# Two cross-attentions: the root and the reciprocal of the image scores' norms as one power on GpSimd

## The chip, the core and the metric

The kernel runs on one core of a Trainium2 chip. The metric is the device time of one execution in microseconds (us), the median of several runs. The engines are named as in the profile: PE is TensorE's matmuls (PEld its weight loads), DVE is VectorE, ACT is ScalarE, POOL is GpSimd and SP is SyncE, which here only issues DMAs. A name such as L864 is line 864 of the kernel before.

## The reference

Two cross-attention layers follow one another on `x` of shape (64, 256, 320): 64 batches, 256 tokens, 20 heads of 16 channels. Each batch has 77 context rows of 512 channels. All arithmetic is float32.

The first layer is a plain softmax attention over all 77 rows. The second layer takes 73 rows as text and the last 4 as image tokens. The text part is a plain softmax attention. The image part adds to its scores a similarity between the context that the text attention has gathered and the image tokens, both divided by their norms:

```python
qsem = jnp.einsum('bhst,bte->bhse', probs_t, text_ehs)
qsem = _l2norm(qsem)            # x / max(sqrt(sum(x * x)), 1e-12)
ip_n = _l2norm(ip_ehs)
sem = jnp.einsum('bhse,bne->bhsn', qsem, ip_n)
fused = attn_scores + 0.5 * sem
probs_ip = jax.nn.softmax(fused, axis=-1) * spatial_mask[None, None, :, None]
out = text_out + probs_ip @ v_ip
```

Each layer ends in a projection, a bias and the residual.

## The kernel before

Everything lies on chip with channels on the partitions. The 64 batches go in 32 pairs p. A pair and layer is cut into ten units: five for each batch b of the pair, each of 128 tokens and eight heads (the last unit of five holds both token halves of the last four heads). One main loop over steps g handles one unit of layer 0 and one unit of layer 1 of an earlier pair (13 steps behind), so that a pair takes ten steps; k = g mod 10 is the place in such a round. The order of the instructions on TensorE, VectorE, ScalarE and GpSimd is the order in which the program writes them: `keep_order` pins it (SP's only up to step 13). Into each step the program puts other work by its k (`fillers`): projections, queries, keys, value rows.

A step does the following.
- TensorE writes one four-bank PSUM tile `sc` (there is only one, so the next step's matmuls wait until the last reader is done): the semantic products of the unit before last of layer 1 (`semantics`, L763 and L770), then the scores of the new units (`scores`, L649).
- VectorE takes the maximum `mx` (L667) and the difference `w` (L669) for each layer, then `prod` (L781, L784) from the semantic products.
- ScalarE takes the exponentials (L677 for layer 0, L680 and L681 for layer 1), copies `sums` out of `sc` (L1048), and copies the transposed weights `pt` and `pr` out of PSUM (L719, L720, L738, L739).
- TensorE transposes the weights (L712, L713).
- VectorE sums and inverts layer 0's weights (`sm`, L694, L695); GpSimd multiplies them (`parts`, L699). GpSimd also copies layer 1's image scores aside (`att`, L684).
- VectorE reduces `prod` to the unit's part of `nrm` (L1121), the squared length of the gathered context. The length itself is never built: the kernel uses a Gram matrix of the context rows, which `gram` (L505 to L511) prepares a batch at a time and sends through DRAM.

With the last unit of a batch, which falls on k = 9 for b = 0 and on k = 4 for b = 1 (the `ends` steps, 64 in all), come the norms of the whole batch, 128 partitions by 40 columns (two token halves by 20 heads):
- `image_squares` (L859, L860, VectorE) bounds the squared length from below; `text_output` (L833 on VectorE, then three products by `by_head`, L851, on GpSimd) scales the text output into `an`.
- At the very end of that step, `image_norm` (L864, L866, ScalarE) takes the square root with a constant factor, and after it one dummy exponential of a single column. An ACT_TABLE_LOAD stands ahead of each.
- In the next step, `image_scores` inverts the root on VectorE (L872) and GpSimd multiplies and adds (`num`, L873, L874).
- One step on, `image_shifted` takes the maximum (`most`, L879, VectorE) and subtracts it (L880, GpSimd), and `image_exponential` (L883) follows. In the third step `image_weights` normalizes (L890 to L892, and L851 again).
- Transposes (L904) and `outputs` (L917, L929) bring the image part into the projection.

`image_norms` (L332 to L340) runs once near the start: it inverts the norms of all image tokens, 128 by 256 columns, into `rip`, by which `gram` scales the image columns (L509). At the start and in the last steps `keep_busy` (L748) has TensorE transpose the identity where it would otherwise pause.

Of the kernel before, what the change touches and what calls it, by code (L numbers as in the profile page):

```python
# [8 lines left out]
F32 = mybir.dt.float32  # L9
AF = mybir.ActivationFunctionType  # L10
ALU = mybir.AluOpType
# [3 lines left out]
H = 20  # L15
# [7 lines left out]
P = 128  # L23
# [25 lines left out]
SCALE = D**-0.5  # L49
SEM = 0.5  # L50
# [21 lines left out]
def tile_two_cross_attentions(ctx: ExitStack, tc: tile.TileContext, a: dict, out: bass.AP):  # L72
# [35 lines left out]
    nc = tc.nc  # L108
# [5 lines left out]
    const = ctx.enter_context(tc.tile_pool(name="const", bufs=1))  # L114
# [192 lines left out]
    rip = const.tile([P, NIP * NB], F32, tag="rip", name="rip")  # L307
# [24 lines left out]
    def image_norms():  # L332
        sq = wkip.rearrange("p k c -> p (k c)")[:, : KE * NIP * NB].rearrange("p (k t) -> p k t", k=KE)
        nc.vector.tensor_mul(sq, cip, cip)
        ps = pms.tile([P, 512], F32, tag="ms", name="ss_ps")
        for k in range(KE):
            nc.tensor.matmul(ps[:, : NIP * NB], ones, sq[:, k, :], start=(k == 0), stop=(k == KE - 1))
        nc.vector.tensor_scalar_max(rip, ps[:, : NIP * NB], EPS * EPS)
        nc.scalar.activation(rip, rip, AF.Sqrt)
        nc.vector.reciprocal(rip, rip)  # L340


# [493 lines left out]
            lasts[p] = big.tile([P, 2, 2, H - HT, D], F32, tag="an_last", name=f"an_last{p}", bufs=1)  # L836
        by_head((an[:, 0], lasts[p][:, :, b], an[:, 1]), sums[:, :, NIP : NIP + D], rec)

    one = const.tile([P, 1], F32, tag="one", name="one")

    def by_head(to, t, factor):

# [18 lines left out]

    def image_norm(p, b):
        r = stats[p, b][2]
        nc.scalar.activation(r, r, AF.Sqrt, scale=(SCALE / SEM) ** 2)  # L864

        nc.scalar.activation(one, r[:, :1], AF.Exp, scale=0.0)  # L866

    def image_scores(p, b):

        att, sums, r = stats[p, b]  # L870
        num = nums[p, b] = small.tile(full, F32, tag="num", name=f"num{p}_{b}", bufs=2)
        nc.vector.reciprocal(r, r)  # L872
        nc.gpsimd.tensor_mul(num, sums[:, :, :NIP], r.unsqueeze(2).broadcast_to(full))  # L873
        nc.gpsimd.tensor_add(num, num, att)  # L874

# [65 lines left out]
    def fillers(k, p):  # L941
# [58 lines left out]
        elif k == 6:  # L1000
# [5 lines left out]
            if p == 0:  # L1006
                add(0, p, image_norms)
            else:
                add(1, p, keys, 1, p, 1)
# [42 lines left out]
    for g in range(NP * NU + LAG + 12):  # L1052
# [66 lines left out]
        if before1:  # L1119
            q, b, u = before1[:3]  # L1120
            nc.vector.tensor_reduce(eight(stats[q, b][2], u), prod, AX.X, ALU.add)  # L1121
            if ends:
                image_squares(q, b)
                text_output(q, b)
                later[g + 1] = [(image_scores, (q, b))]
                middle[g + 2] = (image_shifted, (q, b))
                between[g + 2] = [(image_exponential, (q, b))]
                (early if b else later)[g + 3] = [(image_weights, (q, b))]
# [10 lines left out]
        if ends:  # L1139
            image_norm(*before1[:2])  # L1140
# [54 lines left out]
```

## Time and profile before

| What | Value |
|---|---|
| Median of 3 runs | 2466.0 us (2465.18 to 2466.5) |
| The profiled execution's own time | 2466.13 us |
| Its span in the profile | 2464.4 us, 97472 instructions |
| Mean granted TensorE clock | 0.997 |
| ScalarE: table loads at L864 and L866 | 64 and 64, 1283 ns each |
| ScalarE: root L864, dummy L866 | 64 and 64, mean 237 and 203 ns |
| VectorE: reciprocal L872 | 64, mean 354 ns |

In the profile, "busy" is the time in which an engine executes, and a wait is put down to the instruction that came last of those waited for. A group line reads: line, engine, operation, output<-inputs, shapes, count, then busy us, mean ns of one, and after the second bar the engine's idle time just before such instructions with what ended it. A timeline line reads: start (us from the span's start), us, engine, line, operation, output<-inputs, shapes, count, and in brackets the idle time before it. The chain of work is followed back from the last instruction, at each step to what released it.

### The profile page before, as it was taken

To read this page: it belongs to the slowest core of one execution; us is meant where nothing else is said; L and a number is where in the kernel's file an instruction comes from. 1 tells how busy PE (TensorE), PEld (TensorE's weight loads), DVE (VectorE), ACT (ScalarE), POOL (GpSimd) and SP (SyncE) were. 2 spreads that over 40 slices of the span, in tenths; PEclk is the share of its full clock that TensorE was granted. 3 is DMA by queue.
4 is the path that set the end of the run, shared out by engine and by line. 5 is a ranking of instruction groups with operands and counts; after the bars stand their busy time and mean duration, and the time that the engine had idled before them with its cause. 6 is when DMAs were issued, how large, how long until landed. Compare 5 with 4: busy or idle time off the path is not lost.

```text
span 2464.4 us, 97472 instructions
## 1 busy us (share of the span) xinstructions
PE 2394.9 (97%) x41118; PEld 1848.5 (75%) x41118; DVE 1986.4 (81%) x3673; ACT 1482.6 (60%) x3742; POOL 1207.8 (49%) x2651
## 2 busy tenths in 40 slices
PE   8899999999999999999999999999999999999888
PEld 6677777777777777777777777777777777777666
DVE  3588788888888888888888888888888888888764
ACT  3466666666666665666666666666666666666543
POOL 2455454555445545445555445555455555455532
PEclk9999999999999999999999999999999999999999
DMA  6212111112211112211111211111211111211000
GB/s 177 71 28 59 55 48 49 50 48 59 65 42 47 48 49 58 66 42 48 48 51 54 67 43 47 48 50 54 67 44 47 48 50 54 65 40 35 23 22 25
DMA packets 163447, 128.79 MB, mean 52 GB/s; under 512 B 65860, under 2 KB 146628, under 8 KB 163012
## 3 DMA queue, kind: packets, MB, share of 16 engines
q1 hardware_dynamic: 162148, 121.42, 17.4%
q8 instruction: 325, 5.32, 0.9%
q10 hardware_dynamic: 864, 1.15, 0.2%
q14 instruction: 110, 0.90, 0.1%
HBM read 83.43 MB, written 36.62 MB: 49 GB/s over the span
## 4 chain that ended last, share of the span: by engine, by line
PE 85%; DVE 10%; ACT 3%; issue 1%; POOL 0%; DMA 0%; DVEq 0%; POOLq 0%; SPq 0%; ACTq 0%
PE tr L712 11%; PE sc L763 10%; PE o_ps L537 9%; PE q_ps L537 9%; PE sc L649 7%; PE v_ps L395 4%; DVE w L669 4%; PE sc L770 4%; PE o_ps L622 4%; DVE mx L667 3%; PE k_ps L353 3%; PE pv L798 3%; PE o_ps L547 3%; PE q_ps L565 3%; PE q_ps L547 3%; PE pv L803 2%
## 5 line engine op out<-in xcount | busy, mean ns | idle before, releaser
L667 DVE TENSOR_REDUCE mx<-sc 128x8 f32<-128x584 f32 (+1 forms) x640 | 496.6, 776 | 333.4 <-PE sc L649 331.1
L699 POOL TENSOR_TENSOR parts<-w,sm 128x512 f32<-128x512 f32 (+1 forms) x640 | 441.1, 711 | 513.7 <-ACT parts L681 236.9
L669 DVE TENSOR_TENSOR w<-sc,mx 128x616 f32<-128x616 f32 x640 | 511.8, 800 | 73.1 <-DVE mx L667 1.4
L712 PE MATMUL tr<-ident,parts 128*128 128x128 f32 x2560 | 407.9, 282 | 10.4 <-ACT pt L719 6.4
L719 ACT COPY pt<-tr 128x512 f32<-128x512 f32 x320 | 187.3, 585 | 325.0 <-PE tr L712 325.0
L712 PEld LDWEIGHTS tr<-ident,parts 128*128 128x128 f32 x2560 | 284.2, 140 | 129.7 <-issue 72.8
L677 ACT ACTIVATE w<-w 128x616 f32<-128x616 f32 x320 | 229.9, 718 | 140.5 <-DVE w L669 136.8
L763 PEld LDWEIGHTS sc<-gv,pt 64*64 64x64 f32 x10240 | 233.0, 133 | 104.7 <-ACT sums L1048 51.3
L684 POOL COPY att<-w 128x32 f32<-128x32 f32 x320 | 67.6, 211 | 485.6 <-DVE w L669 485.6
L763 PE MATMUL sc<-gv,pt 64*64 64x94 f32 x10240 | 277.2, 245 | 22.9 <-ACT sums L1048 22.2
L694 DVE TENSOR_REDUCE sm<-w 128x8 f32<-128x616 f32 x320 | 250.9, 784 | 14.4 <-ACT w L677 14.3
L649 PE MATMUL sc<-kbd,q 32*64 32x154 f32 x10240 | 247.3, 293 | 1.1 <-ACT q L592 1.0
L1048 ACT COPY sums<-sc 128x168 f32<-128x168 f32 x320 | 96.6, 302 | 227.6 <-DVE prod L784 225.9
L537 PE MATMUL o_ps<-aT,wo 128*128 128x256 f32 x1024 | 231.8, 379 | 0.7 <-ACT aT L934 0.7
L537 PE MATMUL q_ps<-x,wq 128*128 128x256 f32 x1024 | 231.6, 379 | 0.0
L1121 DVE TENSOR_REDUCE nrm<-prod 128x8 f32<-128x584 f32 x320 | 226.7, 709 | 0.3
L781 DVE TENSOR_TENSOR prod<-sc,parts 128x512 f32<-128x512 f32 x320 | 217.8, 681 | 2.8 <-PE sc L770 2.8
L537 PEld LDWEIGHTS o_ps<-aT,wo 128*128 128x128 f32 x1024 | 189.6, 190 | 24.4 <-ACT aT L934 1.1
L537 PEld LDWEIGHTS q_ps<-x,wq 128*128 128x128 f32 x1024 | 189.6, 190 | 23.1
L680 ACT ACTIVATE parts<-w 128x512 f32<-128x512 f32 x320 | 206.3, 645 | 0.0
L738 ACT COPY pt<-tr 128x512 f32<-128x512 f32 x256 | 150.8, 589 | 67.1 <-PE tr L712 67.0
L395 PE MATMUL v_ps<-wv,cf 128*128 128x320 f32 (+1 forms) x624 | 179.2, 433 | 0.0
(142 smaller groups left out, 4387.0 us busy)
## 6 DMA issues: line engine op xcount, KB each, us to landing
out_dram<-x SPq DMA_DIRECT2D x64, 256.0 KB
x<-in_x_dram SPq DMA_DIRECT2D x31, 512.0 KB
vm<-v_rows SPq DMA_DIRECT2D x64, 160.0 KB
ct<-in_ctx_dram SPq DMA_DIRECT2D x32, 308.0 KB
cf<-in_ctx_dram SPq DMA_DIRECT2D x38, 256.0 KB
vr<-v_rows SPq DMA_DIRECT2D x64, 130.0 KB
v_rows<-vs SPq DMA_DIRECT2D x38, 192.0 KB
vq<-v_rows SPq DMA_DIRECT2D x128, 48.0 KB
```

The source lines that it names most:

```text
L395: nc.tensor.matmul(ps[:n, :C], cfs[i][:, k, :n], wv[l][:, k, :], start=(k == 0), stop=(k == KE - 1))
L537: nc.tensor.matmul(ps[b][:, m, :], w[:, k, m * P : (m + 1) * P], main[:, k, b * S : (b + 1) * S], start=(k == 0 and m == 0), stop=False,)
L649: nc.tensor.matmul(ps[c, r, 2 * T * l : 2 * T * (l + 1)], tokens[rows, c], kbd[rows, part].rearrange("p e t -> p (e t)"), start=start, sto ...
L667: nc.vector.tensor_reduce(mx, sc[:, :, :, :nt], AX.X, ALU.max)
L669: nc.vector.tensor_tensor(w, sc, mx.unsqueeze(3).broadcast_to([P, 4, 2, T]), ALU.subtract)
L677: nc.scalar.activation(w, w, AF.Exp, scale=SCALE)
L694: nc.vector.tensor_reduce(sm, w, AX.X, ALU.add)
L699: nc.gpsimd.tensor_tensor(two[:, 8 * t0 : 8 * t1].rearrange("p (h t) -> p h t", h=8), w[:, :, t0:t1], sm.unsqueeze(2).broadcast_to([P, 8, ...
L712: nc.tensor.transpose(ps[:, i, :], flat[:, i * P : (i + 1) * P], ident)
L763: nc.tensor.matmul(ps[c, i % 2 * 2 + j, at : at + GV], pt[half_rows, i, c], gv[b][half_rows, part, i, :], start=start and i < 2, stop=False,)
L781: nc.vector.tensor_tensor(prod[:, :, :, :M], sm[:, :, :, :M], w[:, :4].rearrange("p (e a) j t -> p (a j) e t", e=2), ALU.mult)
L1121: nc.vector.tensor_reduce(eight(stats[q, b][2], u), prod, AX.X, ALU.add)
```

## The change

The root with the constant factor, the dummy exponential and the reciprocal become one GpSimd instruction, which raises the squared lengths to the power -0.5, given as a tile of constants. It stands where the root stood: at the end of the `ends` step, after that step's GpSimd work. The constant factor moves into `image_norms`, so that `rip` carries it; there the root and the reciprocal stay as they were.

```diff
         nc.vector.tensor_scalar_max(rip, ps[:, : NIP * NB], EPS * EPS)
-        nc.scalar.activation(rip, rip, AF.Sqrt)
+        nc.scalar.activation(rip, rip, AF.Sqrt, scale=(SCALE / SEM) ** 2)
         nc.vector.reciprocal(rip, rip)
...
-    one = const.tile([P, 1], F32, tag="one", name="one")
+    power = const.tile([P, 2 * H], F32, tag="power", name="power")
+    nc.gpsimd.memset(power, -0.5)
...
     def image_norm(p, b):
         r = stats[p, b][2]
-        nc.scalar.activation(r, r, AF.Sqrt, scale=(SCALE / SEM) ** 2)
-
-        nc.scalar.activation(one, r[:, :1], AF.Exp, scale=0.0)
+        nc.gpsimd.tensor_tensor(r, r, power, ALU.pow)
...
         num = nums[p, b] = small.tile(full, F32, tag="num", name=f"num{p}_{b}", bufs=2)
-        nc.vector.reciprocal(r, r)
         nc.gpsimd.tensor_mul(num, sums[:, :, :NIP], r.unsqueeze(2).broadcast_to(full))
         nc.gpsimd.tensor_add(num, num, att)
```

In the order of instructions, ScalarE loses 128 table loads, 64 roots and 64 dummies, VectorE 64 reciprocals; GpSimd gains 64 powers and one memset; TensorE and SP keep theirs, and all others stay in the same order.

## The prediction

> **What bounds the kernel now.** I read the page's first parts, then the chain of work, then the groups by engine, and last the timeline around the edited steps.
>
> ```profile
> PE 2394.9 (97%) x41118; PEld 1848.5 (75%) x41118; DVE 1986.4 (81%) x3673; ACT 1482.6 (60%) x3742; POOL 1207.8 (49%) x2651
> PE 85%; DVE 10%; ACT 3%; issue 1%; POOL 0%; DMA 0%; DVEq 0%; POOLq 0%; SPq 0%; ACTq 0%
> ```
>
> TensorE is busy 97% of the span at a granted clock of 0.9 or more in all 40 slices, and 85% of the chain is its own. A full round of ten steps lasts 72.8 us in the timeline (from one first `sc` matmul to the next tenth). Step 4, where the second batch's norms come due, lasts 8.22 us (1204.31 to 1212.53) and the chain in it is TensorE alone; step 5, after it, lasts 6.2 us and its chain is VectorE: `mx`, `w`, `mx`, `w`, `prod`, ScalarE's `sums`, and back to the matmuls. So what the edit frees on ScalarE counts only where one of these two chains waits for it.
>
> The groups that the edit touches, from the groups by engine with shapes apart:
>
> ```profile
> L864 ACT ACT_TABLE_LOAD x64 | 82.1, 1283 | 1.1
> L866 ACT ACT_TABLE_LOAD x64 | 82.1, 1283 | 1.1
> L872 DVE RECIPROCAL nrm<-nrm 128x40 f32<-128x40 f32 x64 | 22.6, 354 | 2.0 <-ACT one L866 2.0
> L892 POOL TENSOR_TENSOR imx<-imx,smask 128x40 f32<-128x40 f32 x64 | 16.3, 255 | 5.5 <-DVE imx L891 3.0
> L254 POOL TENSOR_TENSOR head_mask<-head_mask 128x2 f32<-128x2 f32 x1 | 0.2, 195 | 0.1
> ```
>
> **Removed.** At 64 places ScalarE loses load, root, load and dummy exponential: 1283 + 237 + 1283 + 203 = 3006 ns, 192 us in all. VectorE loses 64 reciprocals of 354 ns, 22.6 us. That is 9% of the span, and nearly all of it is covered. At the places after step 4, VectorE's `mx` idles 0.38 us for TensorE after the reciprocal's step, so the 0.35 us only lengthens that idle time; at those after step 9 TensorE runs without a gap (0.04 us idle in step 0). The key matmuls at 1215.20 wait 0.32 us for a copy that the load held up, but in a step that VectorE's chain sets, so I count nothing for it (29 such waits, 9.6 us in all; a rival below). What must go on hiding these savings is TensorE's queries and output projections, and at the kernel's two ends that cover is thin:
>
> ```profile
> 148.78 0.41 PE L712 MATMUL tr<-ident,parts 128*128 128x128 f32 x2 [1.51 <-ACT pt L719]
> 2318.59 0.66 PE L712 MATMUL tr<-ident,parts 128*128 128x128 f32 x2 [2.14 <-ACT pt L719]
> 2391.28 0.98 PE L748 MATMUL busy<-ident 128*128 128x128 f32 x7 [2.00 <-ACT pt L719]
> 2440.44 0.63 POOL L851 TENSOR_TENSOR an<-sums,rec 128x256 f32<-128x256 f32 x1
> 2441.34 0.40 DVE L872 RECIPROCAL nrm<-nrm 128x40 f32<-128x40 f32 x1 [2.00 <-ACT one L866]
> 2441.82 0.49 POOL L873 TENSOR_TENSOR num<-sums,nrm 128x160 f32<-128x160 f32 x1 [0.75 <-DVE nrm L872]
> ```
>
> In the first three, TensorE stands idle for the copy `pt`, which stands behind the two loads. What is late next decides each gain.
> - At 148.8: without loads the transposes could start near 147.3, but `sums` ends near 150.95 on VectorE's chain, and the next `sc` starts at 151.32 now. Gain 0.4 us.
> - At 2318.6: the copy could start at 2316.4 instead of 2317.9, and the four transposes, the gram and the value matmuls would not run slowed after the pause (1.09, 1.24 and 1.00 us against 0.60, 0.70 and 0.64 in a full round). Next late is `sums`, which can end at 2320.7; `sc` starts at 2323.23 now. Gain 2.5 us.
> - At 2391.3: the transposes end at 2389.17, the copy starts at 2390.66. Gain 1.4 us.
> - The tail: GpSimd ends `an` at 2441.07 and starts `num` at 2441.82, after load, dummy and reciprocal. That gap of 0.75 us, less some 0.05 for a start on its own engine's result, is 0.7 us given back, and the power, x us long, stands in its place. Everything after it is serial (`most`, the subtraction, four `vip` products on GpSimd, weights, transposes, projection), so the tail changes by x - 0.7.
>
> **Added.** 64 powers of 128x40 on GpSimd, each x us, queued behind the three `an` products at the end of a step; behind it wait, in GpSimd's queue, the copy `att`, the two `parts` products, `num` and the gram's scaling with its DMA on SP. The power itself waits for nothing: the root's input is ready before `rec`, for which `an` already waits. `num` now waits for GpSimd's own result instead of VectorE's.
>
> No row shows GpSimd computing a power. From below: the multiply of the same shape, 0.255 us (L892). From above: as if each of the 40 columns cost what GpSimd's smallest product does, 0.195 us (L254): 7.8 us. Between them: L699's 128x512 takes 1051 ns in the same view, so a column of one multiply costs (1051 - 255) / 472 = 1.69 ns beside a fixed 0.19. I assume some 30 dependent steps a column (logarithm, product, exponential): 30 x 40 x 1.69 ns + 0.19 = 2.2 us. This is an estimate, nearer to the low row, since the fixed part is paid once an instruction. I take x = 2.2 and keep both ends.
>
> Its cover, from the timeline of a full round:
>
> ```profile
> 1214.24 0.63 POOL L851 TENSOR_TENSOR an<-sums,rec 128x256 f32<-128x256 f32 x1
> 1217.88 0.21 POOL L684 COPY att<-w 128x32 f32<-128x32 f32 x1 [3.01 <-DVE w L669]
> 1219.66 1.38 POOL L699 TENSOR_TENSOR parts<-w,sm 128x512 f32<-128x512 f32 x2 [1.57 <-ACT parts L681]
> 1221.57 0.52 POOL L874 TENSOR_TENSOR num<-num,att 128x160 f32<-128x160 f32 x1
> 1223.98 0.31 DVE L879 TENSOR_REDUCE most<-num 128x40 f32<-128x160 f32 x1
> ```
>
> GpSimd is free from 1214.87; less the copy, 4.5 us pass before `parts` is due. If that is overrun, `num` ends 1.9 us ahead of `most`, which sits in VectorE's chain. So up to x = 6.4 us nothing moves, and each microsecond beyond costs 32 times that. After step 9 the same reading gives 4.45 + 1.6, and 0.86 more because TensorE sets that step: 6.9 us. At 2391 the third gain survives to about x = 4.1.
>
> The rest has one answer: one memset of 128x40 at the start lies ahead of a wait of 5.6 us for `kT`; the factor in the image keys' root adds no instruction; the root there keeps its two loads.
>
> **A rule against the change.** No row shows a pause on GpSimd at the first use of an operation. The Trainium skill (GPSIMD Engine Reference, Instruction dispatch) says that the first call of a freshly loaded kernel pays about 6 us for its code. No run here shows it; if it held once, at 148 us, the sum would grow by some 2 us, and if it held at every place, x would be past 8.
>
> **And one that overstates the gain.** After a load that begins at 2316.47 and takes 1.28 us, the next activation starts at 2317.76, 0.01 us later. The skill (ScalarE: Activation LUTs, What ACT_TABLE_LOAD costs) adds a drain of about 1.38 us to each switch, which the trace does not have; by it the freed time would be, as an estimate, some 370 us instead of 192, and as well covered.
>
> **The sum.** The profiled execution took 2466.13 us, 1.7 beside its span of 2464.4; the median of the three is 2466.0. -0.4 - 2.5 - 1.4 + (2.2 - 0.7) = -2.8, so 2466.1 - 2.8 = 2463.3 us. About 0.2%, 4.9 us, is what a measurement of this kernel can tell from no change, so this lies within it.
>
> **Rivals.**
> - GpSimd becomes the bound. Beyond x = 6.4 the late `num` stops `most`, and with it `prod`, `sums` and the next step's matmuls. At x = 7.8: 32 x 1.4 + 32 x 0.9 = 74 us in the rounds, 7.1 in the tail, less 2.9 (the third gain is gone): 2544 us. For it: a power may be computed in many more steps than 30. Against it: that needs some three times my estimate. Chance 0.30; 0.12 of that lies up to x = 7.2, which gives 26 + 10 + 6.5 - 2.9 = 39.7, 2506 us.
> - The freed ScalarE time shows in every round after all. If the 29 waits of the key matmuls (9.6 us) count in full, 2463.3 - 9.6 = 2453.7 us; half of it gives 2458.5. For it: a hidden pause of TensorE may count. Against it: the 0.38 us by which VectorE idles there for the matmuls, while the same chain came to them through `sums`. With the cheapest power alone, x = 0.255, the time is 2461.4. Together 0.17 for a time more than 4.9 us shorter.
> - The change not doing what it says is excluded: by the order of instructions 128 loads, 64 roots, 64 dummies and 64 reciprocals are gone, and each engine keeps the rest in order.
>
> **Numbers.** My forecast, within 0.2%, has 0.53: x between 0.3 and 6.4, its own range 2461 to 2470. The range takes in half of the faster rival and the slower one to x = 7.2: 2458.5 to 2506, which leaves out 0.18 above and a little below.
>
> **What would show it.** No table load but the first three; the power's mean near 2.2 us on GpSimd; rounds of 72.8 us unchanged; TensorE's waits at 148, 2318 and 2391 gone; `num` in the tail later by about 1.5 us relative to `an`. Wrong: a power above 6.4 us, with `most` waiting for `num` in every round, or step 5 shorter than 6.2 us.

## The result and the profile after

The changed kernel is slower: 2488.53 us in the median of 4 runs (2487.58 to 2488.71), against 2465.59 us (2465.15 to 2466.5) for the kernel before beside it. The ratio is 1.0092 [1.0074, 1.0109], a loss of 22.9 us. The forecast was 2463.3 us, no measurable change; the time lies in the range given, on the side of the rival "GpSimd becomes the bound". The profiled execution took 2488.71 us with a span of 2487.0, so 22.6 us more span than before, at a mean granted clock of 0.995 instead of 0.997.

From the page of the changed kernel, the engines' busy times, the shares of the chain that ended last, and the group of the new instruction:

```profile
PE 2396.9 (96%) x41118; PEld 1851.5 (74%) x41118; DVE 1975.4 (79%) x3609; ACT 1297.9 (52%) x3486; POOL 1629.8 (66%) x2716
...
PE 82%; DVE 10%; POOL 5%; ACT 2%; issue 1%; DMA 0%; DVEq 0%; SPq 0%; POOLq 0%; ACTq 0%
...
L865 POOL TENSOR_TENSOR nrm<-nrm,power 128x40 f32<-128x40 f32 x64 | 434.6, 6790 | 0.0
```

ScalarE lost 184.7 us of work and VectorE 11.0; TensorE's stayed within 2 us. GpSimd gained 422 us: one power takes 6.79 us, three times the forecast's 2.2. GpSimd is still busy only two thirds of the span, but it holds 5% of the chain where it held none. The view of waits, for VectorE (waiting line, releaser, then us in total, times, longest us), says where it came in:

```profile
DVE most L877 <- POOL num L872: 22.3, 33, 9.7
DVE w L669 <- POOL att L684: 4.6, 5, 2.4
```

Before, `most` waited for `num` once, 1.2 us in the tail. Now it does 33 times: 9.7 us in the tail, where nothing else is left to do, and 12.6 us over 32 places elsewhere. Of these 32, 29 stand in step 1, after a power of step 9, with 0.37 us each in most rounds; step 1 itself is no longer for it (7.28 us as before). In step 6, after a power of step 4, VectorE idles only some 0.13 us for `num`, and this view counts waits from 0.15 us on. The five waits for `att` are few, but the longest of them, 2.4 us, falls in the last round. The timeline of GpSimd and VectorE in the same full round as in the prediction (the lines are L852 for `an`, L871 and L872 for `num`, L877 for `most` in the changed kernel):

```profile
1220.25 0.63 POOL L852 TENSOR_TENSOR an<-sums,rec 128x256 f32<-128x256 f32 x1
1220.84 6.79 POOL L865 TENSOR_TENSOR nrm<-nrm,power 128x40 f32<-128x40 f32 x1
...
1227.59 0.20 POOL L684 COPY att<-w 128x32 f32<-128x32 f32 x1
1227.76 1.37 POOL L699 TENSOR_TENSOR parts<-w,sm 128x512 f32<-128x512 f32 x2
1229.29 0.80 DVE L669 TENSOR_TENSOR w<-sc,mx 128x616 f32<-128x616 f32 x1
1229.65 0.52 POOL L872 TENSOR_TENSOR num<-num,att 128x160 f32<-128x160 f32 x1
1230.21 0.32 DVE L877 TENSOR_REDUCE most<-num 128x40 f32<-128x160 f32 x1
1230.45 0.68 DVE L781 TENSOR_TENSOR prod<-sc,parts 128x512 f32<-128x512 f32 x1
```

Read it downwards: the power runs from 1220.84 to 1227.6, and the copy, the two `parts` products and `num` follow without a gap. `num` ends at 1230.17 and `most` starts at 1230.21, after VectorE's `w` has ended at 1230.09. Counted from the step's first `sc` matmul, `most` starts at 5.26 us instead of 5.04 in the median of the full rounds. Behind `most`, on VectorE, stands `prod`, which sets when the next step's matmuls start. Before, `num` ended 1.9 us ahead of `most`.

Where the 22.6 us went, from the lengths of the same step in both kernels (a step starts with its first `sc` matmul):

| Place | Change of the span, us |
|---|---|
| Ahead of the first `sc` matmul and in the first two rounds (from -2.0 to +0.5 in sum in the runs below, whatever the edit) | +0.2 |
| The third round, the first behind a power | +1.6 |
| 28 full rounds, 73.13 us instead of 72.77 each in the median | +9.4 |
| The round before the last | +0.8 |
| The last round | +4.0 |
| Tail, after the last `sc` matmul | +6.6 |

In a full round step 6 grew by 0.22 us (6.69 instead of 6.47), step 3 by 0.10, and step 0 by 0.03. Over the 28 rounds that is 5.0 us in step 6 and 3.3 in step 3.

Step 3 pays for the late `num` of step 1. There `most` starts 0.45 us later than before, and VectorE stays that much behind through step 2. So ScalarE's `sums`, and behind it the queries `q` (L579), which the scores of step 3 read, come 0.45 us later in the step. Step 3 before, from its first `sc` matmul at 1195.64, then in the changed kernel, from 1201.56:

```profile
1195.98 0.38 ACT L579 COPY q<-q_ps 128x256 f32<-128x256 f32 x1
1196.61 0.76 PE L649 MATMUL sc<-kbd,q 32*64 32x154 f32 x32
```

```profile
1202.35 0.38 ACT L579 COPY q<-q_ps 128x256 f32<-128x256 f32 x1
1202.53 0.87 PE L649 MATMUL sc<-kbd,q 32*64 32x154 f32 x32
```

Before, `q` is there ahead of the scores; in the changed kernel it ends at 1202.73, in the midst of them, and they take 0.11 us longer.

### The profile page after: what moved, and what is told of

Its sections match the earlier page's. It is cut to its first block, busy times and chain, and to the rows that moved or that the text cites. A ratio compares the mean times of both kernels' runs of the same rounds, so it can differ in the third digit from the quotient of the medians.

```text
span 2487.0 us, 97464 instructions
## 1 busy us (share of the span) xinstructions
PE 2396.9 (96%) x41118; PEld 1851.5 (74%) x41118; DVE 1975.4 (79%) x3609; ACT 1297.9 (52%) x3486; POOL 1629.8 (66%) x2716
## 4 chain that ended last, share of the span: by engine, by line
PE 82%; DVE 10%; POOL 5%; ACT 2%; issue 1%; DMA 0%; DVEq 0%; SPq 0%; POOLq 0%; ACTq 0%
PE tr L712 11%; PE sc L763 10%; PE q_ps L537 9%; PE o_ps L537 8%; PE sc L649 7%; PE v_ps L395 4%; PE sc L770 4%; PE o_ps L622 4%; DVE mx L667 3%; PE k_ps L353 3%; DVE w L669 3%; PE pv L798 3%; PE q_ps L547 3%; PE q_ps L565 2%; PE o_ps L547 2%; PE pv L803 2%
## 5 line engine op out<-in xcount | busy, mean ns | idle before, releaser
L865 POOL TENSOR_TENSOR nrm<-nrm,power 128x40 f32<-128x40 f32 x64 | 434.6, 6790 | 0.0
```

What stands on the lines that cost most here:

```text
L865: nc.gpsimd.tensor_tensor(r, r, power, ALU.pow)
```

## Experiments

The theory: the power is 6.8 us long, GpSimd's queue behind it delivers `num` too late for `most`, and nothing else of the edit matters. Its rivals: the loss comes from ScalarE or VectorE, whose work moved in time; or the cost is in the place in a queue rather than in the length.

**A product in the power's place.** The root is left out of the image norms; all else is the changed kernel.

```diff
-        nc.gpsimd.tensor_tensor(r, r, power, ALU.pow)
+        nc.gpsimd.tensor_tensor(r, r, power, ALU.mult)
```

> The power becomes a product with the same tile: one GpSimd instruction of the same shape in the same place, so the root is left out. Theory 1 (the loss is GpSimd's time in its queue, and only what of it is not covered): the product takes 0.25 us; the rounds go back to 72.77 us, most waits for num no more, the tail loses its 6.6 us, and the time is 2461 to 2465 us. Theory 2 (the loss comes from the rearranged ScalarE work, with pauses of TensorE at the ends): the time stays above 2475 us.

Measured: 2463.28 us against 2465.05, ratio 0.9994 [0.9986, 1.0003]. The group, and the place where the forecast's second gain should have been, in TensorE's timeline:

```profile
L865 POOL TENSOR_TENSOR nrm<-nrm,power 128x40 f32<-128x40 f32 x64 | 17.3, 270 | 0.0
```

```profile
2319.36 0.62 PE L803 MATMUL pv<-pr,vr 104*32 104x256 f32 x8
2322.12 1.09 PE L748 MATMUL busy<-ident 128*128 128x128 f32 x8 [2.15 <-ACT gram L508]
2323.15 0.88 PE L763 MATMUL sc<-gv,pt 64*64 64x94 f32 x32
```

The instruction takes 0.270 us, rounds last 72.79 us, and the tail is 0.08 us shorter than before. So the whole loss is the power's length. With next to no power, what the 192 us of freed ScalarE time and 22.6 us of VectorE time bring can be told in three steps: 0.35 us in the third round, 0.62 in the step at 2318 and 1.38 in the one at 2391. By the interval it is at most 0.14% in all. The round before the last is 2.15 us shorter in the profile, but 1.55 of this is TensorE's clock in its step 7: that step takes 7.83 us at a granted clock of 1.00, where the kernel before has 9.39 at 0.82. It takes 8.06 at 1.00 in the run that moves `most` in the kernel before (below), with all loads in place, and 9.39 with half of the power, so the 1.55 cannot be put down to the freed time. The timeline shows why most of the second of the three gains is not had: TensorE does reach the value matmuls (L803) early, but then `keep_busy` (L748) stands idle 2.15 us for a PSUM buffer that ScalarE's copy `gram` (L508) frees, and the step is only 0.62 us shorter (8.59 instead of 9.21).

**Half of the power.** It covers the first 20 columns only; half of the roots are left out.

```diff
+        nc.gpsimd.tensor_tensor(r[:, :H], r[:, :H], power[:, :H], ALU.pow)
```

> The power on the first 20 of the 40 columns; the other half keeps its squared length, so half of the roots are left out. The power should take about 3.5 us if its price is by the column. Theory 1 (a threshold near 6.4 us): the rounds are 72.77 us, the tail is later by 2.8 us, and the time is 2463 to 2468 us. Rival (the power slows other engines for as long as it runs): half of the loss stays, about 2477 us.

```profile
L865 POOL TENSOR_TENSOR nrm<-nrm,power 128x20 f32<-128x20 f32 x64 | 227.7, 3558 | 0.0
```

Measured: 2466.79 us against 2465.05, ratio 1.0007 [0.9998, 1.0015]. Twenty columns less save 6790 - 3558 = 3232 ns: 162 ns a column, beside 0.33 us a call. At 3.56 us the rounds last 72.80 us: below the forecast's threshold the power costs nothing there. The tail grows by 2.75 us, and the forecast's x - 0.7 gives 2.86.

**The power added to the kernel before.** Loads, roots and reciprocals stay; a power of two constant tiles goes into a tile that nothing reads.

```diff
         nc.scalar.activation(one, r[:, :1], AF.Exp, scale=0.0)
+        nc.gpsimd.tensor_tensor(spare, base, power, ALU.pow)
```

> The kernel before with its root, loads, dummy and reciprocal, and beside them a GpSimd power of the same shape on tiles of constants, in the place that it has in the changed kernel. Theory 1: GpSimd's queue alone makes the loss, so the time is that of the changed kernel, 2488 us, or up to 4 us more for the loads at the ends. Theory 2 (the rearranged ScalarE work makes the loss): 2466 to 2470 us.

Measured: 2484.6 us against 2465.05, ratio 1.0077 [1.0063, 1.0091]; the power takes 6791 ns on constants too, rounds last 73.13 us (step 6 +0.22, step 3 +0.11), and the tail grows by 6.3. The same loss in the rounds with ScalarE and VectorE as before settles that it comes from GpSimd's queue alone. The total is 3.4 us below what was expected, the time of the changed kernel: the last round grew by 1.2 us instead of 4.0. Most of the difference is TensorE's clock there. The changed kernel, then this one, in the timeline of the last round:

```profile
2401.88 6.80 POOL L865 TENSOR_TENSOR nrm<-nrm,power 128x40 f32<-128x40 f32 x1
...
2408.63 0.20 POOL L684 COPY att<-w 128x32 f32<-128x32 f32 x1
2408.87 0.80 DVE L669 TENSOR_TENSOR w<-sc,mx 128x616 f32<-128x616 f32 x1 [2.40 <-POOL att L684]
...
2411.36 1.06 PE L763 MATMUL sc<-gv,pt 64*64 64x94 f32 x32 [2.70 <-ACT sums L1046]
...
2415.16 3.25 PE L748 MATMUL busy<-ident 128*128 128x128 f32 x14 [0.52 <-ACT pt L719]
```

```profile
2408.55 0.80 DVE L669 TENSOR_TENSOR w<-sc,mx 128x616 f32<-128x616 f32 x1 [1.02 <-POOL att L684]
...
2411.04 0.88 PE L763 MATMUL sc<-gv,pt 64*64 64x94 f32 x32 [1.38 <-ACT sums L1054]
...
2413.81 1.75 PE L748 MATMUL busy<-ident 128*128 128x128 f32 x14 [0.62 <-ACT pt L719]
```

In the changed kernel the matmuls come earlier (the third gain), and VectorE's `w` then waits longer for the copy `att`, which stands behind the power: 2.40 us instead of 1.02. For `num`, VectorE waits only 0.25 and 0.26 us after that. By way of `w`, `most`, `prod` and `sums` TensorE pauses for 2.70 us instead of 1.38. After that pause 14 transposes take 3.25 us, here 1.75. The table of stretches (length, then busy us and counts of PE, PEld, DVE, ACT, POOL; then the granted clock, the share of DMA, GB/s) shows the changed kernel's clock first, this kernel's second:

```profile
2411.92:2418.75 6.83, 6.31 (x70) 5.21 (x63) 3.55 (x7) 2.06 (x7) 2.12 (x7) 0.50 0.05 10
```

```profile
2411.10:2417.00 5.90, 5.28 (x143) 4.41 (x151) 4.04 (x8) 3.11 (x9) 2.49 (x9) 1.00 0.08 15
```

So the third gain, 1.38 us in its step, was turned into a longer pause (the next step grew by 2.61 us instead of 1.24), and the slow clock after it added 2.76 us to the step behind.

**Two powers.** A second one of the same shape, on constant tiles, stands right behind the first.

```diff
         nc.gpsimd.tensor_tensor(r, r, power, ALU.pow)
+        nc.gpsimd.tensor_tensor(spare, base, power, ALU.pow)
```

> The changed kernel with a second power of the same shape, on tiles of constants, right behind the first: GpSimd is held for 13.6 us at each of the 64 places. Theory 1 (covered up to about 6.6 us after step 4 and 6.9 us after step 9, every microsecond beyond counts in full): 32 x 6.8 + 32 x 6.7 + 6.8 more, some 2926 us. Rival (the cost grows in proportion to GpSimd's time, 22.9 us for 6.8): 2511 us.

Measured: 2962.29 us against 2465.68, ratio 1.2015 [1.1993, 1.2037], 36 us more than expected. Rounds last 88.6 us: against the kernel before, step 6 grew by 7.4 us, step 1 by 6.6, and steps 2 and 7 by 1.3 and 0.55 in the median. With 13.6 us of power, 13.6 - 7.4 = 6.2 us is the cover after step 4 and 13.6 - 6.6 = 7.0 the one after step 9. The growth of steps 2 and 7 goes with TensorE's clock: its mean is 0.924 here, and after nearly every long pause it is halved for 6.83 us, into the step behind. Two stretches that are both a step 2:

```profile
1140.47:1148.89 8.42, 8.42 (x139) 5.48 (x131) 7.65 (x17) 4.59 (x14) 4.18 (x9) 0.81 0.40 120
1231.35:1238.88 7.53, 7.53 (x138) 4.89 (x131) 7.29 (x15) 4.34 (x12) 4.19 (x9) 0.93 0.48 133
```

Before, such a step takes 7.06 us. It is 1.36 us longer at a clock of 0.81 and 0.47 longer at 0.93. Steps 2 and 7 together cost 44 us in the 28 full rounds, more than the 36 that were not expected. VectorE's waits:

```profile
DVE w L669 <- POOL att L684: 354.3, 63, 9.1
DVE most L881 <- POOL num L876: 112.2, 64, 16.3
```

At this length it is not `num` first that is late but the copy `att`, which is next in GpSimd's queue and reads the buffer that VectorE's next `w` needs, as in the last round of the changed kernel. The forecast named the copy as queued behind the power, but took only `num` as the one who is waited for.

**`most` behind `prod`.** In the changed kernel the block that issues `image_shifted` moves behind the products, so that a late `num` does not hold `prod`.

```diff
-        if g in middle:
-            fn, args = middle.pop(g)
-            fn(*args)
...
         prod = weighted(ps, *before1[:4])
+        if g in middle:
+            fn, args = middle.pop(g)
+            fn(*args)
```

> The changed kernel with the maximum most issued behind prod on VectorE instead of ahead of it; nothing else moves. Theory 1 (in the rounds the late num stops most, and through VectorE's order prod, sums and the next matmuls): step 6 falls from 6.69 us to about 6.2, since prod no longer stands behind most, and the time falls by some 24 x 0.49 + 1.2 = 13 us to about 2475 (2472 to 2479). Rival (it is the late parts product, or the late copy att that holds w, that sets the step): step 6 stays at 6.69 us and the time within 2 us of 2488.

Measured: 2476.27 us against 2465.68, ratio 1.0044 [1.0030, 1.0057]. With the power still 6.79 us long, VectorE waits for `num` only once outside the tail, 0.8 us:

```profile
DVE most L877 <- POOL num L872: 10.5, 2, 9.7
```

Rounds fall from 73.13 to 72.82 us, and the 0.10 us of step 3 are gone too. That shows the wait of `most`, with `prod` behind it, to be the rounds' loss. What stays is the tail, +6.9 us, and 2.1 us in the last round's step 6, where `w` still waits 2.41 us for `att`. The profiled execution is the shortest of the five (2473.67 us), 2.6 below the median, so these lengths do not hold all of the loss that is left.

**The same move in the kernel before.**

> The kernel before with the same move of most behind prod. Theory 1: most's 0.27 us leave VectorE's chain in step 6 (6.47 to 6.2 us), some 25 x 0.27 = 7 us less: 2458 us (2456 to 2461). Rival (step 6 is set elsewhere): no change, 2465 us.

Measured: 2464.79 us against 2465.68, ratio 0.9997 [0.9988, 1.0005]. The 7 us expected are not there. Step 6 did fall by 0.22 us, to 6.25, but step 7 rose from 6.81 to 7.05. Its timeline, from the first `sc` of step 7 to the next:

```profile
1225.76 0.88 PE L763 MATMUL sc<-gv,pt 64*64 64x94 f32 x32
...
1226.34 0.20 DVE L695 RECIPROCAL sm<-sm 128x8 f32<-128x8 f32 x1
...
1226.72 1.38 POOL L699 TENSOR_TENSOR parts<-w,sm 128x512 f32<-128x512 f32 x2 [0.40 <-ACT num L883]
...
1230.76 0.76 POOL L851 TENSOR_TENSOR iw<-num,imx 128x64 f32<-128x64 f32 x3
1230.85 1.03 PE L904 MATMUL itr<-ident,iw 128*80 128x128 f32 x4
...
1232.81 0.88 PE L763 MATMUL sc<-gv,pt 64*64 64x94 f32 x32
```

Here `sm` ends 0.78 us after the step's start, because `most` now stands ahead of it on VectorE; before it ended 0.55 after. With it `parts` and, along GpSimd's queue, the `iw` products come 0.24 us later (5.00 us after the start instead of 4.76), and TensorE's transposes `itr` wait for those. The work of `most` was moved, not taken off the two steps together. This is read from the timeline; no run tests it.

**The power ahead of `an`.** In the changed kernel `image_norm` is issued right after `image_squares`, so that the power starts before the three `an` products, which wait for `rec`.

```diff
         image_squares(q, b)
+        image_norm(q, b)
...
-        if ends:
-            image_norm(*before1[:2])
```

> The changed kernel with the power ahead of the three an products in GpSimd's queue, so that it starts some 1.7 us earlier. Theory 1: 6.8 us is then below the cover (6.6 + 1.7), the rounds go back to 72.8 us, the first round's 1.2 us and 1.7 us of the tail are gone: some 2474 us (2470 to 2478). Rival (the power's length counts, not its place): 2488 us.

Measured: 2479.55 us against 2465.68, ratio 1.0054 [1.0041, 1.0066], above what was expected. The rounds are back at 72.82 us, as expected. The miss is the tail, in GpSimd's timeline:

```profile
2445.76 6.77 POOL L865 TENSOR_TENSOR nrm<-nrm,power 128x40 f32<-128x40 f32 x1 [6.00 <-DVE nrm L861]
2452.50 0.63 POOL L852 TENSOR_TENSOR an<-sums,rec 128x256 f32<-128x256 f32 x1
2453.09 0.41 POOL L852 TENSOR_TENSOR an_last<-sums,rec 128x128 f32<-128x128 f32 x1
2453.45 0.63 POOL L852 TENSOR_TENSOR an<-sums,rec 128x256 f32<-128x256 f32 x1
2454.04 0.49 POOL L871 TENSOR_TENSOR num<-sums,nrm 128x160 f32<-128x160 f32 x1
```

Power and `an` have changed places, but `num` stands behind both in one queue, and GpSimd is free before either: the tail grows by 6.8 us, against 6.6. The last round's 3.7 us stay too: there `w` waits 2.03 us for `att`.

**The last three batches by the root.** `most` behind `prod` as above; 61 batches by the power, the last three as before by ScalarE's root and VectorE's reciprocal.

```diff
-        nc.gpsimd.tensor_tensor(r, r, power, ALU.pow)
+        if 2 * p + b < 2 * NP - 3:
+            nc.gpsimd.tensor_tensor(r, r, power, ALU.pow)
+            return
+        nc.scalar.activation(r, r, AF.Sqrt)
+        nc.scalar.activation(one, r[:, :1], AF.Exp, scale=0.0)
...
+        if 2 * p + b >= 2 * NP - 3:
+            nc.vector.reciprocal(r, r)
```

> The changed kernel with most behind prod, and with the last three batches' norms by ScalarE's root and VectorE's reciprocal as before; the other 61 are still powers on GpSimd of 6.8 us. Theory 1 (what is left of the loss with most behind prod is the last pair's thin cover and the serial tail): the tail loses its 6.9 us and step 6 of the last round its 2 us; with the gains of 1.9 us left in the round before, the time is 2466 us (2464 to 2468), though GpSimd still spends over 400 us on powers. Rival (the powers cost something in every round that the step lengths do not show): above 2472 us.

Measured: 2465.74 us against 2465.93, ratio 0.9999 [0.9990, 1.0008]. From the view of the tile `nrm` (count, then min/median/max ns, first and last start):

```profile
L867 POOL TENSOR_TENSOR nrm<-nrm,power x61: 6788/6792/6797, 147.1 to 2357.8; 128x40 f32<-128x40 f32 x61
```

61 powers of 6.79 us cost nothing that can be measured when `most` does not hold `prod` and the tail has none of them: rounds of 72.80 us, tail +0.02. The kernel before with the same move of `most` has the ratio 0.9997. With that the loss is accounted for by three places: `most` ahead of `prod`, the last round, and the tail; only in the third round 0.8 us of it stay. No version measured beats the kernel before by more than can be told from no change.

## Why the prediction was wrong

- **The step that failed is the term x**, one power on GpSimd. It was put at 2.2 us, as 30 steps a column of 1.69 ns: 51 ns a column. It measured 6.79 us, 162 ns a column, or 96 of those steps. The upper bound, 0.195 us for each column, was the nearer row; the fixed part was small, as assumed. The number of steps had no row behind it, and the forecast's side of zero hung on it.
- **The threshold was right.** It was put at 6.4 us after step 4 and 6.9 after step 9. The runs give 6.79 - 0.22 = 6.57 and 13.6 - 7.4 = 6.2 for the first, 7.0 for the second, and no cost in the rounds at 3.56. After step 4 the mechanism was the rival's: `num`, `most`, `prod`, then the next step's matmuls. After step 9 TensorE does set step 1, but its 0.86 us hide the delay only there: `most` is 0.45 us late, and step 3 pays 0.10 for it by way of `q`, although 6.79 lies below the 6.9.
- **The rival's price was too small.** At x = 6.79 its formula gives 32 x 0.39 + 6.1 - 2.9 = 15.7 us against 22.6. The rounds came out near it, 28 of them at about 0.35, but this is in part luck: 0.22 is the path that the formula has, and 0.10 the one by `q`, which it lacks. What it lacked besides was the kernel's end: +2.6 us in step 6 of the last round, where `w` waits for the copy `att` and not `most` for `num`, and +2.76 for the slow clock in the step behind; and 1.6 us in the third round.
- **The tail was right in its mechanism:** x - 0.7 gives 6.1 at the measured x, and 6.6 was measured; 2.9 against 2.75 at half the length. With the product it gives -0.4, and `num` does start 0.44 us earlier behind `an` (0.31 instead of 0.75), but the tail is only 0.08 shorter.
- **The gains.** The first came in (0.35 us, 0.4 forecast), and the third in its own step (1.38, 1.4 forecast), although x was past the 4.1 put as its limit; but it was lost again in the pause behind it. The second was 0.62 us with the product instead of 2.5: `sums` was named as next late, but it was the copy `gram`, which frees the buffer of the transposes that keep TensorE busy.
- **"The freed ScalarE time shows in every round" is refuted.** With the product rounds are 72.79 us: the 29 waits of the key matmuls were hidden, as argued. The drain that the Trainium skill (ScalarE: Activation LUTs, What ACT_TABLE_LOAD costs) adds to each table switch would have made more time free; the trace of the kernel before does not have it.
- **The rule on a first call was not the reason.** The first power, at 148.5 us, is no longer than the others: all 64 lie between 6771 and 6803 ns, and GpSimd idles 0.0 us ahead of them. The pause of about 6 us that the Trainium skill (GPSIMD Engine Reference, Instruction dispatch) puts on the first call of a freshly loaded kernel is not seen at any of them.

Open is why one power takes 162 ns a column; the runs show that it goes by the column and not by the data. Open is also what the same power would take on VectorE, in the reciprocal's place: no run has a time for it.

## What to carry to other kernels

An engine that is busy half of the time has no free half at any given place: read from the timeline how long its queue may be late there, and who stands behind the one that waits, and who stands ahead of it in the same queue. That threshold could be read to some 0.2 us before any run here; the price of an operation that no row shows cannot, so where the threshold lies between its two bounds, the forecast should give the far side its full weight, or the operation be measured alone first. And time freed on an engine that nobody waits for is worth nothing, however much it is: 192 us of table loads and roots here brought at most 0.14%.

## What the runs showed of the hardware

- GpSimd raises to a power at 162 ns a column of 128 partitions and 0.33 us a call, where its multiply of the same 128x40 takes 0.255 to 0.27 us in all. Constants in place of data make no difference (6791 ns).
- A pause of TensorE can cost more than its length. After 2.70 us without a matmul the granted clock was 0.50 for the 6.83 us shown above. In the changed kernel a pause of 2.14 us, up to 2332.95, before the same `keep_busy` as with the product halved it for 3.41 us; with the product a pause of 2.15 us at this place, up to 2322.12, did nothing. The first three lines are the changed kernel's, the last two those with the product:

```profile
2329.99:2333.41 3.42, 1.28 (x20) 0.71 (x13) 3.17 (x7) 1.94 (x6) 3.42 (x1) 1.00 0.00 0
2333.41:2336.82 3.41, 3.41 (x78) 2.86 (x84) 0.00 (x0) 0.00 (x0) 3.41 (x3) 0.50 0.00 0
2408.51:2411.92 3.41, 0.71 (x30) 0.56 (x32) 2.77 (x6) 0.91 (x3) 3.14 (x10) 1.00 0.02 5
```

```profile
2317.26:2320.67 3.41, 2.27 (x29) 1.57 (x29) 3.17 (x5) 1.84 (x5) 1.88 (x5) 1.00 0.02 5
2320.67:2324.08 3.41, 1.96 (x51) 1.68 (x58) 1.80 (x5) 1.37 (x5) 1.95 (x4) 1.00 0.00 0
```

In these traces the slow clock, half of the full one, comes in stretches of 3.41 us or a whole multiple of it, and within a trace their starts lie on one grid of 3.41 us. The lines are cut on this grid. What differs is where a pause falls on it: each of the two costly pauses lies in one place of the grid and leaves TensorE busy for 1.28 and 0.71 us of it; the harmless one lies across two, which keep 2.27 and 1.96. Over the ten traces, from some 60 us on, no slow stretch begins behind a place that TensorE filled to more than 0.53, and one begins behind every place that it filled to less than 0.42; between the two both happen. The Trainium skill (TensorE: Matmul & The Clock Gate, Part 1) says that the clock is set by how busy TensorE has been, in a window of about 3.4 us that runs freely and is not reset when a kernel starts. The grid agrees with that. So a few microseconds at the end of this kernel depend on where its pauses fall.
